# Keeping the last expert rows of the last batch on chip, in an attention and mixture-of-experts kernel

## The chip, the cores and the metric

The kernel runs on one core of a Trainium2 chip, as one launch. The core has a matrix engine (PE, with its weight loads shown as PEld), a vector engine (DVE), a scalar engine (ACT), GpSimd (POOL) and SyncE (SP), which issues DMAs. The metric is the device time of one execution in microseconds (us), as the median of several runs. Each engine takes its instructions in program order and waits on semaphores for the others.

## What is computed

A batch of four sequences of 512 tokens with 256 features passes through attention, a layernorm, a mixture-of-experts layer and a second layernorm. The layer that the change touches is this one:

```python
logits = x @ gate_w.T
topv, topi = jax.lax.top_k(logits, TOP_K)                 # 8 of 64 experts for each token
rw = softmax(topv)
W = zeros((N, E)).at[arange(N)[:, None], topi].set(rw)
gu = einsum('nh,eih->nei', x, gu_w)
gate, up = gu[..., :I], gu[..., I:]
inter_w = silu(gate) * up * W[:, :, None]
out = einsum('nei,ehi->nh', inter_w, dp_w)
out = out + sigmoid(x @ sh_gate1_w.T) * sh_out            # a shared expert
x = layernorm(x + out)
```

All of it is float32. The reference weighs every expert for every token; the kernel computes only the chosen ones.

## The kernel before

**Tiling.** A sequence is one batch b of 0 to 3; it has NT = 4 tiles of 128 tokens. The 64 experts are taken in 16 quads of four (q, 0 to 15). For one tile an expert has CELL = 32 slots, so for a batch it has SLOTS = 4 x 32 = 128 slots, and the slot is the partition of the quad's result.

**The order.** Everything is written as generators, one for each kind of work: p (project), s (scores), v (context), r (route), h (prepare), g (gather), u (up), d (down), i (fetch), c (combine) and a few small ones. The string ORDER at the top of the file has one letter for each step, and the kernel issues the steps in that order (lines 999 to 1001). The string is thus the program order on every engine; nothing else decides it. A step that stands early in the string and waits holds back what stands behind it on its engine, on that engine alone.

**Route** (line 724) makes the logits of a batch, the best eight by a max instruction, and for each chosen expert the place of the token in the expert's slots. From the place comes `code`, of which prepare and gather make one-hot matmuls that collect the tokens of 16 experts (bf16 in three parts, lines 879 to 883), and `at` (line 774), the eight row numbers of each token. The weights `w8` (lines 804 to 818) come from an exponential `rest`, picked by comparing row numbers (DVE line 808, POOL line 811, DVE line 813), with their sum `sm` for the softmax.

**Up and down.** `up` (line 893) loads the down weights of a quad (`dq`, line 897, on SP, three buffers), multiplies the collected tokens by the gate and up weights (line 907), and makes the activation on ACT and DVE (lines 914 to 916). `down` (line 920) multiplies by the down weights (line 927): the result `ys` has for each of 128 slots four experts with 256 features. ACT copies it from PSUM to `yq` (line 932), and SP stores it to `rows_out[b]` in HBM (line 934), a tensor of 8192 rows of 1 KB, where the row of a slot and an expert is `slot * 64 + expert`.

**Fetch and combine.** For every batch, tile and choice k there is one gather: 4 x 4 x 8 = 128 of them. It is an indirect DMA issued by POOL (line 945) that brings 128 rows of `rows_out[b]`, by the numbers in `at`, into one of RING = 5 buffers `got`. It has a bound check. `combine` (line 952) multiplies the rows by the weight and adds them to the tokens in place (DVE, line 956); this frees the buffer. A gather waits for all 16 stores of its batch, since the tensor is one. After every second tile, combine runs a layernorm over the pair of tiles (line 569; three rounds of Newton's method for the root) and SP stores the result (line 963).

**PSUM.** `double` takes one of three pairs of banks, `single` one of two single banks.

Of the kernel before, what the change touches and what calls it, by code (L numbers as in the profile page):

```python
# [15 lines left out]
P = 128  # L16
# [12 lines left out]
PRB = (2, 1, 1)  # L29

ORDER = (
    "pppppsppspsppppsppvvvsvsvsvvspsvvsvvsvspvsvvsvsvsvvrvvsvsrrvsvvvrhsvrrsvvsrhrsvrsprrphprppshvvvvrgpg"
    "vsvrsvhvpsrvvrrvrsvsvsvvsrsvhhvrsvvsprvsvvhrsrvrsvvgrrpprgvrpsrvgpsvrrrvrsvsvvsvvgrsrrsvvvvrrsrssrrg"
    "vhrvvvvvrgvrvtgggrruuugguugllldrruguduuggggrgdguuduggurrddguuugudgguluggduggghuhduuhdhhuhugduuggdhud"
    "gughugugdrgugdruudugguughidriiigdggcruuccgiuiicciigdggruccicuuiidiggcuuiggccrdiguucccdiugudgrgcuuiig"
    "gcdcugigghhudhuuhdughudghhuuhgduugcgduuiicggdcigcucigiudggciciccuuicggdguuiicdigchcdicuicuiguciuggdc"
    "cciuiudicccguggucicdcgugiccuiidigiuugdccciggicuiuigggcrgidghcuuhdhhuuduhicchgicucdugigiduhuugghcdugu"
    "gdgcuugdcicuuicggiccciduiuiccicidgigugcgiucgidcuicgucciidgcuiugdccgcuiiugdcccgiucgicdgicuugudcgcigcu"
    "iiggiuccciduiuiigccdicugcuccidiguiuicduudcccuciciuducuidiccuiihcidrcciicdiicizzcicicicicccccciiciicc"
    "iciicicicicicicicciiciccccicicicicicicicicicicicccccccc"  # L40
# [363 lines left out]
def kernel(  # L404
# [19 lines left out]

    nc = tc.nc
# [10 lines left out]
    ROWS = SLOTS * NE  # L436

# [16 lines left out]
    def single(name):  # L454
        return ps_s.tile([P, S], FP, tag="s", name=name)
# [41 lines left out]
    rows_out = [dram.tile([ROWS, E], FP, name=f"rows_out{i}") for i in range(B)]  # L497
# [39 lines left out]
    turn_ = const.tile([P, 1], FP, name="turn_")  # L537
    start_ = const.tile([P, 1], FP, name="start_")
    for half in range(2):
        part = slice(PART * half, PART * half + PART)  # L540
        nc.gpsimd.memset(turn_[part, :], 1.0 if half == 0 else -1.0)
        nc.gpsimd.memset(start_[part, :], 0.0 if half == 0 else float(WIDTH + 1))
    number = const.tile([P, NT, NE], FP, name="number")
    for half in range(2):
        part = slice(PART * half, PART * half + PART)
        base = NE * ((CELL - WIDTH) * half - 1) + 1
        nc.gpsimd.iota(
            number[part], pattern=[[CELL * NE, NT], [1, NE]], base=base, channel_multiplier=0,
            allow_small_or_imprecise_dtypes=True,
# [19 lines left out]
    def layernorm(r, name):  # L569

        n = r.shape[1]
        st = small.tile([P, n, 6], FP, tag=f"st{n}", name=f"st_{name}")
# [491 lines left out]
```

## Time and profile before

| what | us |
|---|---|
| median of three runs | 518.9 (517.78 to 519.8) |
| the profiled execution, own time | 567.88 |
| its span, first to last instruction | 565.9 |
| PE busy | 453.8 (80%) |
| DVE busy | 337.2 (60%) |
| ACT busy | 245.5 (43%) |
| POOL busy | 210.1 (37%) |
| start of the last down matmuls | 499.76 |
| the last gather is issued | 551.28 |
| the last store is issued | 558.75 |

The profiled execution took 49 us longer than the median of the runs; positions in the trace (in us from the span's start) belong to this execution. PE's busy time is modelled, and adds up matmuls that overlap only once. A gather's busy time is the time in which POOL writes its descriptors; the data come later. "Issue" is time for which no wait is seen. The mean clock granted to PE was 0.92 of full speed. 82.10 MB were moved by DMA.

### The profile page before, as it was taken

The numbers are of one execution on the slowest core, as the hardware profiler recorded it, in microseconds if no ns is written. First come the engines' busy times: TensorE is split into PE (matmuls) and PEld (weight loads), VectorE is DVE, ScalarE is ACT, GpSimd is POOL, SyncE is SP. The second block draws the span as 40 slices with busy tenths as digits, with TensorE's granted clock in tenths as the row PEclk, the third lists the DMA queues.
The fourth block names the chain that finished last, engine by engine and source line by source line (L and its number), as shares of the span: only waits on it lengthen the run. The fifth ranks groups of instructions, "written<-read, shape, count | busy, mean of one in ns | idle before, by whom it ended". The sixth has DMA issues, their size and how long they took to land.

```text
span 565.9 us, 12367 instructions
## 1 busy us (share of the span) xinstructions
PE 453.8 (80%) x4873; PEld 308.8 (55%) x4873; DVE 337.2 (60%) x944; ACT 245.5 (43%) x446; POOL 210.1 (37%) x233
## 2 busy tenths in 40 slices
PE   4999999999999899999879799978997876930000
PEld 2554554645555577787657586756784655720000
DVE  2233377786776884566557575665784655575543
ACT  1438666557555444565435464343553423220000
POOL 6215323433332400000563305544316354466770
PEclk9999999999999999999998899997999989885555
DMA  8700000000000085765665477673776665673331
GB/s 256 297 0 2 1 2 1 1 2 1 1 1 2 2 296 208 274 228 195 200 203 190 162 238 244 211 274 123 240 257 228 217 228 186 213 262 103 103 114 38
DMA packets 31907, 82.10 MB, mean 145 GB/s; under 512 B 4704, under 2 KB 10336, under 8 KB 30816
## 3 DMA queue, kind: packets, MB, share of 16 engines
q1 hardware_dynamic: 25696, 64.44, 32.8%
q0 software_dynamic: 6144, 16.79, 9.9%
q8 instruction: 40, 0.66, 0.5%
q14 instruction: 27, 0.22, 0.1%
HBM read 45.55 MB, written 35.65 MB: 144 GB/s over the span
## 4 chain that ended last, share of the span: by engine, by line
PE 71%; issue 7%; ACT 6%; another core or an unknown queue 5%; DVE 4%; DMA 4%; POOL 1%; POOLq 0%; SPq 0%; ACTq 0%; DVEq 0%
PE gu L907 21%; PE px L879 11%; PE y L927 10%; PE sT L653 7%; PE av L681 6%; PE pq L612 3%; PE po L715 3%; PE pk L612 3%; PE pv L626 3%; DMA got<-rows_out,at 2%; ACT pr L658 2%; PE pt_c L694 2%; ACT xt L869 2%; PE pl L736 1%
## 5 line engine op out<-in xcount | busy, mean ns | idle before, releaser
L945 POOL DMA_INDIRECT got<-rows_out,at x128 | 131.7, 1029 | 198.6 <-DVE x L956 99.7
L907 PE MATMUL gu<-xt,gu_sb 128*64 128x128 f32 x2048 | 136.2, 286 | 4.0 <-issue 3.9
L907 PEld LDWEIGHTS gu<-xt,gu_sb 128*64 128x64 f32 x2048 | 118.6, 143 | 25.5 <-issue 24.4
L658 ACT ACTIVATE pr<-sT 128x768 f32<-128x768 f32 (+1 forms) x96 | 79.3, 880 | 41.7 <-PE sT L653 41.7
L663 POOL TENSOR_SCALAR_AFFINE_SELECT pr<-pr 128x512 f32<-128x512 f32 x64 | 41.6, 661 | 109.2 <-ACT pr L658 109.2
L932 ACT COPY yq<-y 128x1024 f32<-128x1024 f32 x64 | 64.8, 1014 | 37.0 <-PE y L927 27.5
L956 DVE SCALAR_TENSOR_TENSOR x<-got,w,x 128x256 f32<-128x256 f32 x128 | 62.4, 488 | 26.3 <-DMA got<-rows_out,at 23.5
L927 PE MATMUL y<-dq,ma 64*128 64x256 f32 x512 | 72.7, 398 | 0.3 <-issue 0.2
L915 DVE SCALAR_TENSOR_TENSOR ma<-ma,gu 128x256 f32<-128x256 f32 x64 | 26.7, 418 | 73.1 <-ACT ma L914 62.5
L914 ACT ACTIVATE ma<-gu 128x256 f32<-128x256 f32 x64 | 24.6, 384 | 98.6 <-PE gu L907 42.6
L879 PE MATMUL px<-hot,xh 64*128 64x320 bf16 x256 | 40.8, 309 | 28.2 <-ACT xt L869 25.3
L869 DVE COPY xt<-px 128x512 f32<-128x512 f32 x64 | 43.8, 685 | 26.0 <-ACT xt L869 20.2
L869 ACT COPY xt<-px 128x192 f32<-128x192 f32 (+1 forms) x128 | 46.4, 375 | 26.0 <-PE px L879 17.8
L927 PEld LDWEIGHTS y<-dq,ma 64*128 64x128 f32 x512 | 48.3, 194 | 9.7 <-issue 4.5
L653 PE MATMUL sT<-qT,kT 32*128 32x128 f32 (+3 forms) x512 | 51.8, 467 | 0.5 <-ACT pr L658 0.5
L879 PE MATMUL px<-hot,xl 64*128 64x320 bf16 x256 | 41.0, 305 | 1.5 <-issue 1.5
L879 PE MATMUL px<-hot,xm 64*128 64x320 bf16 x256 | 40.5, 304 | 2.0 <-issue 2.0
L681 PE MATMUL av<-pr,va 128*32 128x128 f32 (+3 forms) x512 | 40.3, 438 | 0.3 <-POOL pr L663 0.3
L879 PEld LDWEIGHTS <-xh 64*128 64x128 bf16 x256 | 14.5, 95 | 46.1 <-issue 43.8
L653 PEld LDWEIGHTS sT<-qT,kT 32*128 32x128 f32 x512 | 24.0, 183 | 18.6 <-issue 11.7
L811 POOL TENSOR_TENSOR pick<-pick,rest 128x512 f32<-128x512 f32 x16 | 20.5, 1280 | 32.5 <-DVE pick L808 28.8
L916 DVE TENSOR_TENSOR ma<-gu,ma 128x256 f32<-128x256 f32 x64 | 27.1, 424 | 2.2
(116 smaller groups left out, 484.0 us busy)
## 6 DMA issues: line engine op xcount, KB each, us to landing
rows_out<-yq SPq DMA_DIRECT2D x64, 512.0 KB
dq<-in_dp_dram SPq DMA_DIRECT2D x64, 256.0 KB
gu_sb<-in_gu_dram SPq DMA_DIRECT2D x8, 1024.0 KB
x<-in_x_dram SPq DMA_DIRECT2D x4, 512.0 KB
got<-rows_out,at POOLq DMA_INDIRECT x128
out_dram<-x SPq DMA_DIRECT2D x8, 256.0 KB
wq_sb<-in_wq_dram SPq DMA_DIRECT2D x1, 256.0 KB
wk_sb<-in_wk_dram SPq DMA_DIRECT2D x1, 256.0 KB
```

The costliest lines, as they stand in the source:

```text
L612: nc.tensor.matmul(ps, w_sb[n][:, kc, c * P : (c + 1) * P], xT[:, kc, :], start=(kc == 0), stop=(kc == KC - 1),)
L653: nc.tensor.matmul(s_ps[r // 2][:, r % 2, lo : lo + widths[m]], kTs[b][rows, c, kb * P : (kb + 1) * P], qTs[b][rows, c, par, kb * P :], st ...
L658: nc.scalar.activation(pr[:, 2 * i : 2 * i + 2, :], s_ps[i][:, :, : sum(widths)], AF.Exp, scale=1.0 / HD**0.5)
L663: nc.gpsimd.affine_select(out=pr[:, :, lo : lo + P], in_=pr[:, :, lo : lo + P], pattern=[[0, 4], [1, P]], compare_op=ALU.is_ge, fill=0.0, ...
L681: nc.tensor.matmul(av[32 * r : 32 * r + 32, kb * P :], vas[b % 2][:, kb, 8 * c + 2 * r + par, :], pr[:, r, lo : lo + w], start=(kb == 0), ...
L869: copy(xt[:, kc, :, t * CELL + lo : t * CELL + hi], ps[:, kc, lo * GROUP : hi * GROUP].rearrange("p (s e) -> p e s", e=GROUP),)
L879: nc.tensor.matmul(ps[:, kc, first : first + WIDTH * GROUP], parts[b][i][PART * half : PART * half + PART, t, kc * P : (kc + 1) * P], o[PA ...
L907: nc.tensor.matmul(gu_ps[64 * e : 64 * e + 64, j, which, :], gu_sb[p // GUC][:, p % GUC, kc, which, 64 * e : 64 * e + 64], xt[:, kc, QUAD ...
L927: nc.tensor.matmul(ys[:, e, j, :], a[64 * e : 64 * e + 64, j, :], dq[64 * e : 64 * e + 64, j, :], start=True, stop=True,)
L932: nc.scalar.copy(yq.rearrange("s j e h -> s e j h"), ys)
L945: nc.gpsimd.indirect_dma_start(out=g, out_offset=None, in_=rows_out[b], in_offset=bass.IndirectOffsetOnAxis(ap=ats[b][:, t, k : k + 1], ax ...
L956: nc.vector.scalar_tensor_tensor(acc[:, t, :], got.pop(n), w8s[b][:, t, k : k + 1], acc[:, t, :], ALU.mult, ALU.add)
```

## The change

The last batch's last LATE = 5 quads (20 experts, q 11 to 15) are no longer stored to HBM and gathered. Their rows stay in SBUF, and a matmul adds them to the tokens. In detail:

- `rows_out` of batch 3 has only the 44 x 128 = 5632 rows of quads 0 to 10 (SOON). The row number is now `(quad * 128 + slot) * 4 + expert in the quad` in every batch, so that a quad's store is one contiguous half megabyte. Row numbers of batch 3 are clamped to SOON - 1, and the weights of the late experts are set to zero for the gathers. All 32 gathers of the batch remain.
- `route` of batch 3 makes a dense weight for all 64 experts, the total of them for the softmax (in place of `sm`), and for the late experts a pair (weight, slot number). The pair is transposed by PE, copied by ACT and written to a small HBM tensor `spread` by SP.
- `weigh` (w) reads `spread` back with four broadcasting DMAs, so that the 32 slots of each tile stand on 32 partitions with all weights and slot numbers of the tile's tokens, and DVE makes the weighted one-hot matrix `wide` in five steps.
- `down` copies a late quad into the space of the first gate and up weights, which batch 3 has used by then, and stores nothing.
- `collect` (k) multiplies `wide` by the kept rows, 80 matmuls with 32 rows, 128 columns and 256 moving columns, into two pairs of PSUM banks, and DVE adds the four results to the tokens.
- Every gather goes without a bound check.
- In batch 3 the layernorm runs over tiles 0 to 2 and then over tile 3 alone, where one operation per Newton round is merged away, and the stores of batch 3 are issued by ACT.
- ORDER is a new string throughout, 872 steps in place of 855. Ahead of the down step of batch 3's quad 10 stand 94 gathers, where it was 85; ahead of its quad 15 stand 113, where it was 94. Behind the last down step there are 15 gathers, where it was 34.

```diff
@@ ORDER: all lines replaced, the end of the string:
-    "iciicicicicicicicicciiciccccicicicicicicicicicicicccccccc"
+    "kwduuciiiciciducikddckicciwwikcizcciccckkkciiiiicciikcczccicccccikcicccc"
...
-    rows_out = [dram.tile([ROWS, E], FP, name=f"rows_out{i}") for i in range(B)]
+    rows_out = [dram.tile([ROWS if i < B - 1 else SOON, E], FP, name=f"rows_out{i}") for i in range(B)]
+    spread = dram.tile([2, NT, EL, P], FP, name="spread")
...
+        if n == 1:
+            nc.vector.tensor_scalar(ve, ve, -0.5, None, ALU.mult)
         for _ in range(3):
-            nc.vector.scalar_tensor_tensor(step, rstd, -0.5, rstd, ALU.mult, ALU.mult)
-            nc.vector.tensor_tensor(step, step, ve, ALU.mult)
+            if n == 1:
+                nc.vector.scalar_tensor_tensor(step, rstd, ve[:, 0:1], rstd, ALU.mult, ALU.mult)
+            else:
+                nc.vector.scalar_tensor_tensor(step, rstd, -0.5, rstd, ALU.mult, ALU.mult)
+                nc.vector.tensor_tensor(step, step, ve, ALU.mult)
             nc.vector.scalar_tensor_tensor(rstd, step, 1.5, rstd, ALU.add, ALU.mult)
...
-            nc.vector.scalar_tensor_tensor(row, place, float(NE), number, ALU.mult, ALU.add)
+            nc.vector.scalar_tensor_tensor(row, place, float(QUAD), number, ALU.mult, ALU.add)
...
-            nc.vector.tensor_scalar(at, near, ROWS - 1.0, None, ALU.min)
+            nc.vector.tensor_scalar(at, near, (ROWS if b < B - 1 else SOON) - 1.0, None, ALU.min)
...
+            if b == B - 1:
+                dense = lg[:, :, 0:NE]
+                nc.vector.tensor_tensor(dense, rest, chosen, ALU.mult)
+                total = small.tile([P, NT, 1], FP, tag="total", name="total", bufs=1)
+                nc.vector.tensor_reduce(total, dense, AX.X, ALU.add)
+                nc.vector.reciprocal(total, total)
+                nc.vector.memset(rest[:, :, FIRST:], 0.0)
+                yield
...
+                nc.vector.scalar_tensor_tensor(
+                    pair[:, :, 0, :], dense[:, :, FIRST:], 0.5, total.to_broadcast([P, NT, EL]), ALU.mult, ALU.mult
+                )
+                nc.vector.tensor_scalar(pair[:, :, 1, :], code[:, :, FIRST:], shift_[:, 0:1], None, ALU.add)
+                pt = single("pt_pair")
+                for t in range(NT):
+                    nc.tensor.transpose(pt[: 2 * EL, t * P : (t + 1) * P], pair[:, t].rearrange("p w e -> p (w e)"), ident)
...
+                nc.scalar.copy(flip[: 2 * EL, :], pt[: 2 * EL, :])
+                for which in range(2):
+                    nc.sync.dma_start(
+                        out=spread[which].rearrange("t e k -> e t k"),
+                        in_=flip[EL * which : EL * (which + 1), :].rearrange("e (t k) -> e t k", t=NT),
+                    )
+                yield
...
+            if b == B - 1 and q >= NQ - LATE:
+
+                n = q - (NQ - LATE)
+                yq = gu_sb[n // 2].rearrange("p g k w i -> p (g k w i)")
+                yq = yq[:, (n % 2) * QUAD * E : (n % 2 + 1) * QUAD * E]
+                nc.scalar.copy(yq.rearrange("s (j e h) -> s e j h", j=2, e=2), ys)
+                kept[n] = yq.rearrange("s (e h) -> s e h", h=E)
+                yield
+                continue
...
-            dst = rows_out[b].rearrange("(s e) h -> s e h", e=NE)
             nc.sync.dma_start(
-                out=dst[:, q * QUAD : (q + 1) * QUAD, :], in_=yq.rearrange("s j e h -> s (j e) h")
+                out=rows_out[b].rearrange("(q s e) h -> q s (e h)", s=SLOTS, e=QUAD)[q],
+                in_=yq.rearrange("s j e h -> s (j e h)"),
             )
+            yield
+
+    def weigh():
+
+        wide = hots["wide"] = late["pool"].tile([P, 2, EL, P], FP, tag="wide", name="wide")
+        for t in range(NT):
+            nc.sync.dma_start(
+                out=wide[CELL * t : CELL * (t + 1)],
+                in_=spread[:, t][None].to_broadcast([CELL, 2, EL, P]),
+            )
+        nc.vector.tensor_scalar(lane, lane, CELL - 1, None, ALU.bitwise_and)
+        nc.vector.tensor_copy(slot_, lane)
+        yield
+        for n in range(LATE):
+            part = slice(n * QUAD, (n + 1) * QUAD)
+            nc.vector.scalar_tensor_tensor(
+                wide[:, 0, part], wide[:, 1, part], slot_[:, 0:1], wide[:, 0, part], ALU.is_equal, ALU.mult
+            )
+            yield
+
+    def collect():
+
+        acc = [double(f"acc_{i}") for i in range(2)]
+        for n in range(LATE):
+            for e in range(QUAD):
+                for t in range(NT):
+                    rows = slice(CELL * t, CELL * (t + 1))
+                    nc.tensor.matmul(
+                        acc[t // 2][:, t % 2, 0:E], hots["wide"][rows, 0, n * QUAD + e, :], kept[n][rows, e, :],
+                        start=(n == 0 and e == 0), stop=(n == LATE - 1 and e == QUAD - 1), skip_group_check=True,
+                    )
+            yield
+        for t in range(NT):
+            part = xs[B - 1][:, t, :]
+            nc.vector.tensor_tensor(part, acc[t // 2][:, t % 2, 0:E], part, ALU.add)
             yield
...
-                bounds_check=ROWS - 1, oob_is_err=False,
+                bounds_check=None, oob_is_err=True,
...
-            if t % 2 and k == TOP - 1:
-                part = slice(t - 1, t + 1)
+            ends = (1, 3) if b < B - 1 else (2, 3)
+            if t in ends and k == TOP - 1:
+                part = slice(0 if t < 3 else ends[0] + 1, t + 1)
                 yield from layernorm(acc[:, part, :], f"2_{b}_{t}")
-                nc.sync.dma_start(
+                (nc.sync if b < B - 1 else nc.scalar).dma_start(
                     out=out[b].rearrange("(t p) e -> p t e", p=P)[:, part, :], in_=acc[:, part, :]
                 )
```

## The prediction

> **What bounds the kernel now.** I read the page's slices first, to see which engine is full where. The rows are PE, POOL and the clock granted to PE, each digit a tenth of a slice of 14.1 us.
>
> ```profile
> PE   4999999999999899999879799978997876930000
> POOL 6215323433332400000563305544316354466770
> PEclk9999999999999999999998899997999989885555
> ```
>
> PE is nearly full for 36 slices and empty in the last four, where POOL is at its fullest: the end is a stretch without matmuls, some 57 us long. What fills it is in the costliest groups (busy, mean ns of one, then idle before it):
>
> ```profile
> L945 POOL DMA_INDIRECT got<-rows_out,at x128 | 131.7, 1029 | 198.6 <-DVE x L956 99.7
> L932 ACT COPY yq<-y 128x1024 f32<-128x1024 f32 x64 | 64.8, 1014 | 37.0 <-PE y L927 27.5
> L956 DVE SCALAR_TENSOR_TENSOR x<-got,w,x 128x256 f32<-128x256 f32 x128 | 62.4, 488 | 26.3 <-DMA got<-rows_out,at 23.5
> ```
>
> Then the chain that ended last, around the last matmul (start, length, what):
>
> ```profile
> 499.76 1.23 PE y L927 x8
> ...
> 501.06 1.02 ACT yq L932
> ...
> 502.10 3.70 DMA rows_out<-yq
> 505.80 0.04 POOLq L945
> ```
>
> The last quad's rows are copied (1.02) and stored (3.70), and only then may batch 3's gathers start: rows_out is one tensor for a batch. The timeline dates them (start, length, idle before):
>
> ```profile
> 507.57 1.00 POOL L945 DMA_INDIRECT got<-rows_out,at  x1 [0.30 <-issue]
> ...
> 551.28 1.00 POOL L945 DMA_INDIRECT got<-rows_out,at  x1 [0.30 <-issue]
> ```
>
> These are the first and the last of its 32. They go 1.30 us apart (1.00 and 0.30 of issue), so 31 steps are 40.3 us; the other 3.4 of the 43.7 are stalls. After the last: landing and combine to 554.70, layernorm to 558.75, and the store and the end to 565.9: 14.6 us. The waits from 495 us on agree: DVE waits 22.2 us for gathers there, POOL 7.4 us for DVE. **The end is set by when batch 3's rows are complete, plus 32 gathers on POOL, plus 14.6 us.**
>
> Last, the waits between batch 2's last quad (copy at 422.92) and batch 3's quad 10 (copy at 485.72):
>
> ```profile
> POOL got L945 <- DVE x L956: 20.8, 9, 5.6
> DVE ma L915 <- ACT ma L914: 18.2, 5, 4.9
> ```
>
> POOL has room in this stretch (32.5 us busy in 62.8), and waits for ring buffers that DVE frees.
>
> **What the skill says.** Perfetto Trace Analysis, "DMA Instruction — SWDGE (GPSIMD)": the profiled window of such a DMA is the making of descriptors and not the transfer. The trace agrees: the last gather's window ends at 552.28, its combine starts at 554.22. TensorE: Matmul & The Clock Gate, "Part 1: The HAM clock gate": an idle PE falls back to half clock; the page has 0.5 in the tail. There, "Part 3: Packing small matmuls": four row tiles of 32 run at once, measured 3.07 times faster. DMA: Bandwidth & Descriptors, "Issuing engines are not separate DMA queues": another issuing engine saves only its issue time, 0.37 us for the last store here.
>
> **The change, part by part**, against the profiled execution (567.88 us, span 565.9).
>
> *Gate.* Batch 3's gathers now need quads 0 to 10 alone. Quad 10's store was issued at 486.75; with the 3.70 of the chain its rows lie at 490.45 instead of 505.80: **-15.3 us**. The five quads behind it (PE work 14.3 us of that stretch) move beside gathers. Five yq stores go; their copies, 1.01 each, stay.
>
> *Backlog.* That needs batch 2's 32 gathers out of the way. By the order string, 94 gathers stand ahead of the down step of quad 10, where before it was 85 (94 before stood ahead of quad 15). From batch 2's last rows (422.9 + 1.0 + 4.7 = 428.6) to 490.45 there are 61.9 us for 32 x 1.30 = 41.6. It fits, but nine more combines (4.4 us of DVE) and closer gathers lie among the evictions that PE waits for. I take **+2**, bounds -2 and +25 (below).
>
> *Gathers beside matmuls.* In the stretch the combines stand on DVE among ma, weighting and layernorms; a late one holds its ring buffer (five) and so POOL. Between 485.7 and 501 POOL lost 10 us this way, but then it had no haste. I take **+2.5**, bounds 0 and 8.
>
> *No bound check.* Each gather has one 29 ns register move on POOL's queue. If that alone goes, 32 x 0.03 = **-1**; if the whole 0.30 of issue goes, -9.6. No row shows a gather without it, so the lower bound is 0. I take -1.
>
> *Weights by route.* Per the nearest rows: a product and a reduction (0.43 each by L768's median), small ones at 0.18, four transposes of 0.28, one copy of 0.58, two SP stores of about 0.4 issue: some 3 us on DVE, 1 on PE, in batch 1's stretch. DVE is 60 to 66% busy there (windows 250 to 350). The two stores wait for the copy, with dq loads and row stores behind them on SP; dq has three buffers. **+0.5**, bounds 0 and 3; without that cover, about 3.
>
> *weigh.* Four broadcast loads (2.6 MB, what the five stores no longer write), then 5 x 0.7 = 3.5 us of DVE (price of L808, 128x512 with two inputs). DVE is 55% busy in the tail: 0, bounds 0 and 3.5.
>
> *collect.* 80 matmuls of 256 columns with 32 rows. L653, the same tile height, took 51.8 us for 81,920 columns, 0.63 ns each: 20,480 columns are 13 us, or 26 at half clock. Two of five groups stand ahead of the last quad. PE ends at 501 now, so at about 514 with collect, or 527 at half clock, and the end is later by 25 us or more: 0. What waits for it is four DVE additions (0.42 each). The first stand ahead of the 23rd of the 32 gathers, due at about 492.5 + 22 x 1.3 = 521; PE coming later than that would hold the combines behind them. Two of three PSUM pairs are taken meanwhile, so the last four quads alternate matmuls (0.9) with copies (1.0): hidden as well. Upper bound 6.
>
> *End.* Tile 3 is normalised alone: one statistics pass, one aggregation and one scaling fewer (0.33, 0.11, 0.33) and two small operations fewer (2 x 0.2): **-1.2**. The store is half as large, from ACT: 0, bounds -1 and +0.5.
>
> Sum: -15.3 + 2 + 2.5 - 1 + 0.5 - 1.2 = **-12.5 us**. The unprofiled runs have a median of 518.9, 49 us below the profiled execution; I can't place that difference. ACT's 3.5 us wait on an unknown queue in the moved stretch may be part of it, then the gate is worth 12. The cadence of gathers and of quads should hold, so I subtract the sum as it is: **506.4 us**.
>
> **The rivals.**
> - *Backlog rules.* Batch 2's gathers, not quad 10, set the start: the ring stalls of 20.8 us in that stretch stay, and 41.6 + 20.8 = 62.4 exceeds the 61.9 there are; in runs whose quads are quicker by a fifth, the gate comes some 12 us earlier and the backlog doesn't. Left is 2 to 8 us of gain: 511 to 516. For it: those stalls. Against: POOL was waiting for combines that stood late in the order, and the order is new.
> - *Cheap gathers.* Without the check the cadence falls by 0.2 or more, 32 times, 6 us on top: 496 to 499. For it: the 0.30 between two gathers is unexplained. Against: the one visible move is 29 ns.
> - *Slower: combines starve PE.* With gathers back to back a combine waits for its data 0.8 us, as in the tail (1.30 less 0.48); thirty of them are 25 us on DVE, ahead of the evictions of PE's PSUM. If PE loses over 1.3 us per quad in the eleven quads, 14 us, the gain is gone; at all 25, about 518.9 - 14.5 + 25 = 529. Against: up to 495 us DVE waited for gathers only 1.3 us in all.
> - *No change*: the losses just cancel the gate.
>
> **How the numbers follow.** A measurement tells 0.5% (2.6 us) from no change. The forecast (499 to 511) has 0.62; cheap gathers 0.10; backlog 0.13; no change 0.05; slower 0.10. Faster is the first three, 0.85. From 496 to 515 lies all of the forecast, nearly all of the cheap gathers and most of the backlog: 0.81. The forecast's own range is 499 to 511.
>
> **What would show it.** Right: POOL gathering batch 3 while PE still does y and gu; some 15 gathers after the last y (32 before); gathers 1.27 to 1.30 apart; batch 3's first gather soon after quad 10's store; 13 us from the last gather to the end; collect's groups done before the additions are due. Wrong: DVE waiting for gathers while PE idles before the last quad (combines starve PE); batch 3's first gather long after quad 10's rows lie there (backlog); additions waiting for PE at half clock; a cadence well under 1.2 (cheap gathers). A shift in the attention part, whose order string is new too and which I price at nothing, would also make it wrong.

## The result

| | median us | range | runs |
|---|---|---|---|
| before | 518.90 | 516.19 to 521.17 | 9 |
| changed | 515.22 | 512.76 to 516.60 | 9 |

The ratio is 0.9934, with a 95% interval of 0.9905 to 0.9963. The change makes the kernel faster by 3.7 us (0.7%), not by 12.5. The sign was right; the size was not, and 515.22 lies just above the range's upper end of 515.

One fact about the chips has to be told first. The same kernel before takes 519 us in some sets of runs and 561 to 567 us in others. The trace behind the prediction (567.88 us) is of the second sort, the times are of the first. That is the 49 us that the prediction could not place. Below, a chip is *of the first kind* where the kernel before takes 519 us and *of the second kind* where it takes 561 to 567. Whether the kind belongs to the chip for good is not known: the record gives the chips numbers, and number 2 stands for sets of both kinds (518.9 us in two, 566.1 in a later one), which may be one chip or two. Each ratio was measured on a single chip. For the first kind there is also a trace of the unchanged kernel, labelled "before, traced again", with a span of 516.1 us.

The slices of the changed kernel, first kind, one digit for 12.9 us:

```profile
PE   3999999989999989999999999999975969886700
POOL 8041412362335322000016722365633257667751
PEclk9999999999999999999999999999998899998955
```

The empty tail has shrunk to two slices, as intended. But in the 30th to 33rd slices (373 to 425 us) PE falls to 7, 5, 9 and 6. In the kernel before, traced again, it was busy 29.6 of the 30 us from 375 to 405; here 21.9. The groups (busy, mean ns of one, then idle before it):

```profile
L1033 POOL DMA_INDIRECT got<-rows_out,at x128 | 125.1, 978 | 159.9 <-DMA dq<-in_dp_dram 72.1
L1044 DVE SCALAR_TENSOR_TENSOR x<-got,w,x 128x256 f32<-128x256 f32 x128 | 62.8, 491 | 33.0 <-DMA got<-rows_out,at 31.6
L985 ACT COPY yq<-y 128x1024 f32<-128x1024 f32 x59 | 59.7, 1013 | 48.0 <-PE y L971 35.6
```

A gather is 49 ns shorter (1027 ns in the trace of before on the first kind). Next, the first and the last of batch 3's 32 gathers on the timeline. The kernel before, traced again:

```profile
459.49 1.00 POOL L945 DMA_INDIRECT got<-rows_out,at  x1 [0.76 <-DVE x L956]
...
501.80 0.99 POOL L945 DMA_INDIRECT got<-rows_out,at  x1 [0.30 <-issue]
```

The changed kernel:

```profile
460.11 0.94 POOL L1033 DMA_INDIRECT got<-rows_out,at  x1 [2.42 <-DMA dq<-in_dp_dram]
...
503.84 0.95 POOL L1033 DMA_INDIRECT got<-rows_out,at  x1 [0.30 <-issue]
```

**Batch 3's first gather starts no earlier than before**, although it now needs quad 10 alone. Quad 10 itself has moved. The copy of its rows in the kernel before, traced again, and in the changed kernel:

```profile
434.69 1.01 ACT L932 COPY yq<-y 128x1024 f32<-128x1024 f32 x1 [0.73 <-PE y L927]
```

```profile
454.57 1.01 ACT L985 COPY yq<-y 128x1024 f32<-128x1024 f32 x1 [0.72 <-PE y L971]
```

Times in us from the span's start; "small loads" is an experiment below:

| | before, again | changed | small loads |
|---|---|---|---|
| batch 2's quad 5 copied | 353.56 | 356.18 | 356.21 |
| batch 2's quad 10 copied | 374.05 | 373.57 | 374.53 |
| batch 3's quad 10 copied | 434.69 | 454.57 | 446.41 |
| batch 3's quad 15 copied | 453.73 | 481.51 | 474.71 |
| first gather of batch 3 | 459.49 | 460.11 | 452.05 |
| last gather | 501.80 | 503.84 | 495.15 |
| span | 516.06 | 514.76 | 505.81 |

In the kernel before, 19.0 us lay between quad 10 and quad 15. In the changed kernel quad 10 comes 19.9 us later, so the whole gate is used up. What is left is the end: from the last gather to the span's end it was 14.3 us and is 10.9.

The chain of the changed kernel shows where part of it went (start, length, what):

```profile
383.55 1.01 ACT yq L985
...
384.59 13.34 DMA rows_out<-yq
...
398.03 1.02 ACT yq L985
...
399.10 2.08 PE y L971 x8
```

A row store takes 13.34 us to land; in the prediction's chain it took 3.70. Meanwhile ACT can't copy the next quad, since both yq buffers are taken, and PE waits for PSUM. Ahead of this store, at 375.5 to 377.4, stand the four loads of `weigh`:

```profile
wide<-spread SPq DMA_DIRECT2D x4, 640.0 KB, 11.2
```

That is 2.62 MB, and the prediction had priced it at nothing.

### The profile page after: what moved, and what is told of

It reads as the page before. It is cut to its first block, busy times and chain, and to the rows that moved or that the text cites. A ratio compares the mean times of both kernels' runs of the same rounds, so it can differ in the third digit from the quotient of the medians.

```text
span 514.8 us, 12588 instructions
## 1 busy us (share of the span) xinstructions
PE 446.6 (87%) x5037; PEld 306.5 (60%) x5037; DVE 343.7 (67%) x957; ACT 246.4 (48%) x447; POOL 204.3 (40%) x236
## 2 busy tenths in 40 slices
DMA packets 31688, 82.20 MB, mean 160 GB/s; under 512 B 4708, under 2 KB 10500, under 8 KB 30340
## 4 chain that ended last, share of the span: by engine, by line
PE 59%; DMA 19%; DVE 10%; ACT 6%; issue 4%; POOL 1%; SPq 0%; POOLq 0%; DVEq 0%; ACTq 0%
DMA got<-rows_out,at 15%; PE gu L951 14%; PE sT L669 7%; PE y L971 7%; PE av L697 7%; PE px L923 7%; PE pv L642 3%; PE po L731 3%; PE pq L628 3%; ACT pr L674 3%; DMA rows_out<-yq 3%; PE pk L628 2%; DVE x L1044 2%; PE pt_c L710 2%; POOL got L1033 1%
## 5 line engine op out<-in xcount | busy, mean ns | idle before, releaser
L1033 POOL DMA_INDIRECT got<-rows_out,at x128 | 125.1, 978 | 159.9 <-DMA dq<-in_dp_dram 72.1
L951 PE MATMUL gu<-xt,gu_sb 128*64 128x128 f32 x2048 | 126.5, 277 | 1.5 <-DVE xt L913 1.0
L951 PEld LDWEIGHTS gu<-xt,gu_sb 128*64 128x64 f32 x2048 | 111.1, 137 | 20.6 <-issue 16.1
L985 ACT COPY yq<-y 128x1024 f32<-128x1024 f32 x59 | 59.7, 1013 | 48.0 <-PE y L971 35.6
L971 PE MATMUL y<-dq,ma 64*128 64x256 f32 x512 | 71.4, 398 | 12.5 <-ACT yq L985 4.1
L971 PEld LDWEIGHTS y<-dq,ma 64*128 64x128 f32 x512 | 46.8, 192 | 23.6 <-issue 6.1
L913 DVE COPY xt<-px 128x512 f32<-128x512 f32 x64 | 43.7, 684 | 17.9 <-ACT xt L913 17.8
L923 PE MATMUL px<-hot,xh 64*128 64x320 bf16 x256 | 39.4, 302 | 11.5 <-ACT xt L913 5.7
L923 PE MATMUL px<-hot,xl 64*128 64x320 bf16 x256 | 39.0, 298 | 0.0
L923 PE MATMUL px<-hot,xm 64*128 64x320 bf16 x256 | 38.9, 297 | 0.0
L697 PEld LDWEIGHTS av<-pr,va 128*32 128x32 f32 x512 | 13.9, 109 | 26.5 <-issue 18.4
```

The lines of the kernel that those rows point to most:

```text
L697: nc.tensor.matmul(av[32 * r : 32 * r + 32, kb * P :], vas[b % 2][:, kb, 8 * c + 2 * r + par, :], pr[:, r, lo : lo + w], start=(kb == 0), ...
L913: copy(xt[:, kc, :, t * CELL + lo : t * CELL + hi], ps[:, kc, lo * GROUP : hi * GROUP].rearrange("p (s e) -> p e s", e=GROUP),)
L923: nc.tensor.matmul(ps[:, kc, first : first + WIDTH * GROUP], parts[b][i][PART * half : PART * half + PART, t, kc * P : (kc + 1) * P], o[PA ...
L951: nc.tensor.matmul(gu_ps[64 * e : 64 * e + 64, j, which, :], gu_sb[p // GUC][:, p % GUC, kc, which, 64 * e : 64 * e + 64], xt[:, kc, QUAD ...
L971: nc.tensor.matmul(ys[:, e, j, :], a[64 * e : 64 * e + 64, j, :], dq[64 * e : 64 * e + 64, j, :], start=True, stop=True,)
L985: nc.scalar.copy(yq.rearrange("s j e h -> s e j h"), ys)
```

## The experiments

The theory after the result (**bytes**): the loads stand among transfers that the quads need, and delay the gate. The rival (**order**): the new string puts combines and other DVE work among the evictions, and PE waits for those. Before this was clear there were other suspects: the burst, the pace of POOL, and the bound check.

**First runs, chips of the second kind.** The kernel before, unchanged, for its trace:

> The kernel before once more, unchanged, to have a trace of it beside the changed kernel's. Theory: the 49 us by which its profiled execution exceeded its runs were waits of ACT on an unknown queue (37 us in the first trace) between 250 and 500 us; without them the last down matmuls end near 455 us, the tail of 65 us stays as it was (gathers 1.30 us apart), and the span is about 517 us. Rival: the tail itself is shorter in an ordinary run, below 55 us, and PE ends later than 462.

It took 565.43 us. The changed kernel with hardly any load (the string has one letter w more, for the memset, ahead of the first down step):

```diff
         wide = hots["wide"] = ...
+        nc.gpsimd.memset(wide, 0.0)
+        yield
         for t in range(NT):
-            nc.sync.dma_start(out=wide[CELL * t : CELL * (t + 1)], in_=spread[:, t][None].to_broadcast([CELL, 2, EL, P]))
+            nc.sync.dma_start(out=wide[CELL * t : CELL * (t + 1), :, 0:1],
+                              in_=spread[:, t, 0:1][None].to_broadcast([CELL, 2, 1, P]))
```

> The changed kernel with 0.13 MB in place of the 2.6 MB that weigh loads: only one of 20 experts is read back, the rest of the weights is filled with zeros by POOL while it idles, so the late experts' part is left out of the output. Theory (the burst): the four loads hold up the row stores behind them, which stopped PE for about 8 us and slowed batch 3's first quads; without them 502 to 507 us. Rival (the backlog of gathers): the end is set by 64 gathers of batches 2 and 3 on POOL and in the ring, and the burst is absorbed; 513 to 515.

The loads apart (a `yield` behind each load, and the letters w behind the down steps 31, 35, 39 and 43):

> The changed kernel with its four weigh loads (0.66 MB each) issued one at a time, behind the down steps 31, 35, 39 and 43, in place of all four at once behind step 43. Same bytes. Theory (the burst): what hurts is that a store waits behind four loads; apart, each delays a store by under 3 us, which two buffers cover: 504 to 509 us. Rival (the bytes): DMA is so full in this stretch that 2.6 MB more cost 8 to 10 us wherever they stand: 513 to 517. Rival (the backlog): 513 to 515 as well, together with the small load.

The bound check put back:

```diff
-                bounds_check=None, oob_is_err=True,
+                bounds_check=(ROWS if b < B - 1 else SOON) - 1, oob_is_err=False,
```

> The changed kernel with the bound check of the gathers put back. In the traces a gather took 0.998 us with it and 0.95 without (medians), both with 0.30 between. Theory: 0.05 us on each of the 32 gathers at the end, so 1.6 us longer, 516 to 518. Rival: off the path, since gathers in the ring wait for their data anyway: within 0.5 us of 515.2.

The changed kernel itself, and the loads apart once more:

> The changed kernel itself. The first four runs fell on a chip on which the kernel before takes 565 us, not 518.9, and in whose trace PE's semaphore increments arrive 3 to 15 us late while POOL issues gathers one after another. If this call falls on such a chip, theory: the changed kernel is slower than before by about 1%, 569 to 573, since it puts more back to back gathers beside matmuls; rival: it gains its 4 us there too, 560 to 562. On a chip like the one of the result: 513 to 517 against 519.

> The four loads of weigh one at a time (behind the down steps 31, 35, 39 and 43), once more, beside the unchanged changed kernel. On a chip like the one of the result: theory (the burst), 504 to 509; rivals (the bytes, or the backlog), 513 to 517. On the other kind of chip the order of the two should be the same, with less between them, since late increments hide part of it.

| kernel | us | ratio to before (95%) |
|---|---|---|
| small loads | 570.14 | 1.0072 (1.0048 to 1.0097) |
| loads apart | 569.89 | 1.0085 (1.004 to 1.0131) |
| bound check back | 571.95 | 1.0109 (1.0037 to 1.018) |
| changed kernel, second chip | 566.94 | 1.0094 (1.0056 to 1.0132) |
| loads apart, second chip | 567.58 | 1.0107 (1.0039 to 1.0176) |

All five are alike within their intervals, and slower than before. The changed kernel, faster by 0.7% on the first kind, is slower by 0.9% here. Its trace on such a chip shows a wait that the first kind doesn't have. One of ACT's waits over the span, then PE, POOL and ACT on the timeline:

```profile
ACT ma L958 <- remote: 34.4, 5, 14.0
```

```profile
500.18 3.94 PE L951 MATMUL gu<-xt,gu_sb 128*64 128x128 f32 x64
```

```profile
503.13 0.94 POOL L1033 DMA_INDIRECT got<-rows_out,at  x1 [0.30 <-DVE st L586]
...
514.50 0.94 POOL L1033 DMA_INDIRECT got<-rows_out,at  x1 [0.30 <-issue]
```

```profile
517.35 0.38 ACT L958 ACTIVATE ma<-gu 128x256 f32<-128x256 f32 x1 [13.97 <-remote]
```

The trace has the end of PE's gate and up product at 504.12. ACT, which waits for it, starts at 517.35. In the 13.2 us between, POOL issues gathers back to back, and PE's semaphore increment for this product is on record only at 517.33, behind the last of them. PE itself is slow there: collect's next 32 matmul records run from 504.05 to 518.54, 14.5 us, and the same group takes 2.01 on the first kind. So it isn't told whether the increment alone is late or PE as a whole is held up, and that the gathers are the cause is not shown. "Remote" is the trace's word for a releaser that it does not find. The kernel before has the same on the second kind (ACT ma waits 37.1 us for "remote" in the prediction's trace, 30.9 in the one taken here). On the first kind neither trace has one such wait. That five kernels which differ in loads and check come out alike here may be because this waiting covers what they differ in; no run separates the two. What was asked had to be asked on the first kind.

**POOL's pace, and the loads apart, first kind.** One small memset behind each gather, meant to slow POOL down; then the loads apart; and the kernel before for its trace:

```diff
                 bounds_check=None, oob_is_err=True,
             )
+            nc.gpsimd.memset(idle, 0.0)
             yield
```

> The changed kernel with one more POOL instruction, a memset of 128x1, behind each of its 128 gathers. On a chip like the one of the result: POOL takes 0.1 to 0.3 us more for each gather; if the cadence of gathers sets the end (theory of the backlog), the last 32 to 64 of them make it 4 to 12 us longer; if the ring, DVE or PE do (rival), it stays within 2 us. On a chip like the two of the first runs: theory, PE's increments pass in the pauses, and the kernel comes down from 567 towards 530; rival, they wait for something else than POOL's series, and it stays at 567 to 575.

> The four loads of weigh one at a time, for the third time; wanted on a chip like the one of the result. There: theory (the burst), 504 to 509; rivals (the bytes, or the backlog), 513 to 517. On the other kind of chip as before: the same as the changed kernel.

> The kernel before, unchanged, for its trace on this chip. If before is at 519 here, theory: its last down matmuls end near 455 us and its tail is about 60 us; the last gather is issued some 45 us behind the last down step. Rival: PE ends later than 462, and the tail is shorter than 55 us.

The memset: 514.6, ratio 0.993 (0.9907 to 0.9954), as without it. But it slowed nothing: its 0.12 us fell into the 0.30 between two gathers, and their starts still lie 1.25 apart in its trace, so the run doesn't tell whether POOL's pace sets the end. Whether a longer pause lets PE's increments pass on the second kind was not tried there. The loads apart: 517.22, ratio 0.9969 (0.995 to 0.9989), no better than in one burst (0.9934, and the intervals overlap). Quad 10 is copied at 454.00, where in one burst it was 454.57. Row stores took 5.35 us on average to land from 330 to 374 (4.09 in the changed kernel), dq loads 6.90 (4.73): the harm is spread, not gone. So it is not the burst as such that costs. The kernel before took 517.96.

**The loads, taken out, moved, and put alone into the kernel before; first kind, on one chip.**

> The changed kernel with 0.13 MB read back in place of the 2.6 MB (one late expert of twenty has its weights, the others are multiplied by zeros, so that the late experts' part is left out); the order string, the gathers and the matmuls are the same. Where the kernel before takes 519 us: if the bytes of the four loads hold back the transfers that the matmuls wait for (theory: bytes), quad 10 of batch 3 is copied some 9 us earlier than in the changed kernel, at about 445, and the time is 505 to 509 (ratio to before 0.973 to 0.981). If the new order with its earlier combines is what delays the matmuls (rival: order), nothing moves: 513 to 516, ratio 0.99 to 0.996. Where before takes 561 to 565, the late semaphore increments of PE cover both: 1.005 to 1.01.

For the second, only the string differs: the load's w stands behind the down step 59 (batch 3's quad 10), the five DVE steps and collect behind it; the two letters w that stood ahead of that step are gone from there.

```diff
@@ ORDER, from the d of quad 10 on
-diiigggucidcicicicccciciuuciciccwiuuccikwduuciiiciciducikddckicciwwikcizcciccckkkciiiiicciikcczccicccccikcicccc
+dwiiigggucidcicicicccciciuucicicciuucciduuciiiciciduciwdwdkwckicciwkiwckizcciccckkkciiiiicciikcczccicccccikcicccc
```

> The changed kernel with the four loads moved behind the down step of quad 10, and the five steps of DVE and the groups of collect moved behind them; nothing is left out. Theory (bytes): the loads no longer stand among the transfers that the quads need before the gate, so quad 10 is copied at about 445 as without the loads, batch 3's first gather starts at 449 to 452, and the time is 505 to 510, unless the additions of collect come later than the combines that stand behind them, which would cost up to 5. Rival (order): quad 10 stays at 452 to 455 and the time at 513 to 517. Where before takes 561 to 565: a ratio of 1.0 to 1.01.

The third adds four such loads to the kernel before, from a stretch of x, ahead of the down step 44:

```diff
+    def load():
+        wide = late["pool"].tile([P, 20, E], FP, tag="wide", name="wide")
+        for t in range(NT):
+            nc.sync.dma_start(out=wide[CELL * t : CELL * (t + 1)],
+                              in_=x[0, 20 * t : 20 * t + 20, :][None].to_broadcast([CELL, 20, E]))
+        yield
```

> The kernel before with four broadcasting loads of 640 KB each added ahead of the down step of batch 2's quad 11, where the changed kernel has them; what they bring is not used. Theory (bytes): 2.6 MB at the 270 to 280 GB/s that move in this stretch are 9.4 us; the transfers take 85% of the DMA engines there, so the quads up to quad 15 of batch 2 come 6 to 10 us later and the time is 525 to 529 (ratio 1.012 to 1.02). Rival (order): the buffers hide the loads, and the time is 518 to 520.5 (ratio 0.998 to 1.003). Where before takes 561 to 565: a ratio of 1.0 to 1.015 by the theory.

| kernel | us | ratio to before (95%) |
|---|---|---|
| small loads | 507.07 | 0.9774 (0.9735 to 0.9813) |
| loads behind quad 10 | 517.71 | 0.9985 (0.9959 to 1.001) |
| before, with the loads added | 535.00 | 1.0295 (1.0259 to 1.033) |

Without the loads the changed kernel takes 507.07, 0.7 us from the forecast. The loads are worth 1.6% (0.9934 less 0.9774), 8.3 us, or 5.8 to 10.8 with both intervals; in the traces quad 10 moves by 8.2. The wait behind the store is gone. ACT's copies, first in the changed kernel, then with small loads:

```profile
386.76 1.00 ACT L985 COPY yq<-y 128x1024 f32<-128x1024 f32 x1
398.03 1.01 ACT L985 COPY yq<-y 128x1024 f32<-128x1024 f32 x1 [7.87 <-DMA rows_out<-yq]
```

```profile
387.74 1.00 ACT L985 COPY yq<-y 128x1024 f32<-128x1024 f32 x1
391.23 1.01 ACT L985 COPY yq<-y 128x1024 f32<-128x1024 f32 x1
```

Put alone into the kernel before, the loads cost 16.5 us, more than the 6 to 10 expected. PE stood still for one dq load that stood behind them. Its waits from 375 to 412:

```profile
ACT yq L932 <- PE y L927: 19.1, 5, 16.7
...
PE y L927 <- DMA dq<-in_dp_dram: 14.9, 1, 14.9
```

The bytes alone, 2.62 MB at 270 to 280 GB/s, would be 9.4 us by the estimate made ahead of the run. That the rest comes from the order in the queue is argued, not shown. The Trainium skill, DMA: Bandwidth & Descriptors, "Queues, rings and completion order", says that SP's transfers stand in one ring per DMA engine and are taken from it in order, and that an engine serves the rings of different issuers in turn. The trace fits the first: dq loads issued at 374 to 404 took 17.97 us on average to land, 4.51 without the added loads. But POOL's gathers, in another ring, slowed nearly as much, from 4.25 to 14.56, so the trace doesn't tell the order in a ring from a plain lack of room on the DMA engines. A load from another ring was not tried.

Behind quad 10 the loads hurt as much, in another place. The gate did move (quad 10 copied at 445.42, first gather at 451.12), but the next eight gathers took 18.5 us where with small loads they took 10.2. The waits from 450 to 472:

```profile
PE y L971 <- DMA dq<-in_dp_dram: 16.1, 1, 16.1
DVE x L1044 <- DMA got<-rows_out,at: 12.5, 5, 7.1
```

My expectation of 505 to 510 was wrong there: I had taken the stretch behind the gate for an idle one, and it holds the gathers that set the end.

**Half the bytes, and the matmul steps' order; first kind, on one chip.** Slot and weight become one number, slot plus weight, and a weight is below one:

```diff
-                nc.vector.tensor_scalar(pair[:, :, 1, :], code[:, :, FIRST:], shift_[:, 0:1], None, ALU.add)
+                nc.vector.scalar_tensor_tensor(pair, code[:, :, FIRST:], shift_[:, 0:1], pair, ALU.add, ALU.add)
...
-                in_=spread[:, t][None].to_broadcast([CELL, 2, EL, P]),
+                in_=spread[t][None].to_broadcast([CELL, EL, P]),
...
+        nc.vector.tensor_scalar(slot_, slot_, -1.0, None, ALU.mult)
...
-                wide[:, 0, part], wide[:, 1, part], slot_[:, 0:1], wide[:, 0, part], ALU.is_equal, ALU.mult
+            nc.scalar.activation(wide[:, part], wide[:, part], AF.Relu, bias=slot_[:, 0:1], scale=1.0)
+            nc.vector.scalar_tensor_tensor(wide[:, part], wide[:, part], 1.0, wide[:, part], ALU.is_lt, ALU.mult)
```

> The changed kernel with slot number and weight added up to one number (slot plus weight), so that the four loads bring 1.31 MB in place of 2.62; ACT takes the own slot off with a Relu and DVE keeps what is below one. Nothing is left out and the order string is the changed kernel's. Theory (bytes): the loss scales with the bytes, so half of the 8 us between the changed kernel and the one with small loads comes back: 510 to 512 where before takes 519 (ratio 0.983 to 0.988); quad 10 of batch 3 copied at about 450. Rival: what costs is the first burst or the count of loads, and the time stays at 514 to 516 (ratio 0.991 to 0.995). Where before takes 561 to 565: 1.0 to 1.01 by either.

The second kernel mixes the strings: the start up to the first down steps and h, g and u from the string of before (but for one h, ten down steps earlier), fetch, combine, weigh, collect and the last steps of route from that of the changed kernel.

> As the kernel with half the bytes, with the order string mixed: prepare, gather-matmul, up and down steps (h, g, u) stand between the down steps as in the kernel before; fetch, combine, weigh, collect and the last steps of route stand between them as in the changed kernel. It tells where the other 11 to 12 us before quad 10 come from (quad 10 at 446 without the loads, 435 in the kernel before). If they come from the arrangement of the matmul steps, quad 10 comes at 438 to 441 and the time is 500 to 505 where before takes 519 (ratio 0.964 to 0.973). If they come from the earlier gathers and combines beside matmuls, quad 10 stays near 450 and the time is within 2 us of the half-bytes kernel (510 to 513), or above where the mixed string fits its buffers worse. Where before takes 561 to 565: 0.99 to 1.01.

**Half the bytes take 509.17 us, ratio 0.9807 (0.9768 to 0.9846): faster than both kernels, and nothing is left out.** Half the bytes cost only 0.33% (0.9807 less 0.9774), 1.7 us, where in proportion to the bytes it would be 4. With both intervals the cost may be anything up to 4.6, so that the loss grows faster than the bytes is suggested and not shown. The traces point the same way: quad 10 is copied at 446.41 with small loads, 448.93 with half the bytes and 454.57 with all. That buffers hide the loads up to some amount would fit; no run shows it. The kernel with half the bytes also has one store less, and ACT has five steps more. Its four loads of 320 KB landed in 7.1 to 8.6 us, the four of 640 KB in the changed kernel in 9.3 to 17.2.

The mixed order took 528.15, ratio 1.0212 (1.0165 to 1.0259), beyond the numbers of both expectations; the second had left room for a string that fits its buffers worse. ACT waits 13.8 us for DVE's `left` of prepare between batch 2's quad 5 and 15, where the kernel with half the bytes waits 4.4. The mixture made a delay of its own, so it settles nothing on the order.

**The picks early, all of it early.** In the half-bytes kernel the last steps of batch 3's route (r 58 to 62) are moved behind the down steps 25 to 33. In the second kernel, r 54 to 57 also go behind the steps 8 to 12, r 58 to 62 behind 18 to 28, and the loads behind step 15.

> The half-bytes kernel with one thing moved in the order string: the last five steps of route for batch 3 (four picks with their sums, 1.4 us of DVE each, and the scaling) stand behind the down steps 25, 27, 29, 31 and 33, at 300 to 335 us, where they stood behind 37, 43, 48, 50 and 57. In the trace of the kernel with small loads PE idles 10.8 us between batch 2's quad 5 and batch 3's quad 10, where before it idled 2.4, and DVE does 72.3 us of work there where before it did 61.3. If this DVE work ahead of the gate is what PE waits for (theory), the 5.6 us moved out bring 3 to 5 us: 504 to 506.5 where before takes 519 (ratio 0.971 to 0.977). If the waits come from where the combines stand (rival), or from the DMA queues, nothing comes of it: 508 to 510 (0.979 to 0.984). Where before takes 561 to 565: 0.99 to 1.01 by either.

> As the kernel with the picks early, and more: batch 3's weights and pair (route steps 54 to 57) stand behind the down steps 8 to 12, the picks behind 18 to 28, and the four half-size loads behind step 15, at 260 to 270 us, where the DMA engines are busy 70% and no gather runs yet. Theory (bytes and cover): the loads then hold back nothing that the end waits for; beside the gain of the picks another 1.5 to 2.5 us: 502 to 505 (ratio 0.968 to 0.974), with a bend of up to 2 us at batch 0's quad 15. Rival: the loads cost the same there, since PE is full and waits for the same stores and weights: as the kernel with the picks early, within 1 us. Where before takes 561 to 565: 0.99 to 1.01.

> The half-bytes kernel with the four picks and the scaling of batch 3's weights moved to 300 to 335 us, once more, for a chip where the kernel before takes 519. Theory (the DVE work ahead of the gate is what PE waits for): 504 to 506.5, ratio 0.971 to 0.977. Rival (place of the combines, or the queues): 508 to 510, ratio 0.979 to 0.984. Where before takes 561 to 567 the first try gave 1.017, and another such result tells nothing on this question.

> The kernel with the picks, the pair and the half-size loads early (260 to 270 us), once more, for a chip where the kernel before takes 519. Theory: 502 to 505, ratio 0.968 to 0.974. Rival: within 1 us of the kernel with the picks early alone. Where before takes 561 to 567 the first try gave 1.027.

Both tries fell on chips of the second kind: 1.0171 (1.0121 to 1.0221) and 1.0196 (1.0164 to 1.0228) for the picks, 1.0267 (1.0221 to 1.0312) and 1.0287 (1.0248 to 1.0326) for all early. On such a chip they come out worse than the changed kernel (1.0094, 1.0056 to 1.0132), the first of them only at the edge of the intervals. In the second trace with the picks early one of PE's increments again comes 13.6 us late beside gathers issued back to back. On the question that they were made for they say nothing.

## Why the prediction was wrong, point by point

**The failed step: weigh's loads at 0.** The prediction put it as "2.6 MB, what the five stores no longer write". The total is indeed the same (82.10 and 82.20 MB). But the stores left the stretch from quad 11 on, and the loads came into batch 2's quads 10 to 15, ahead of the gate, where the DMA engines were busy 80% and row stores and dq loads stand behind them that PE needs. Cost: 8.3 us, shown by the small loads. The prediction named a bound for weigh (0 to 3.5) and put only DVE's work into it. For the loads it gave neither a place nor cover, although the string says that they stand between batch 2's quad 10 and 11. Added up from the two traces of the first kind, the gate is worth -19.0 us (quad 10 to quad 15 in the kernel before); the loads cost 8.2 and the rest of what delays quad 10 costs 11.7; from quad 10's copy to the first gather it is 0.2 less, the 31 steps of the gathers are 1.4 longer and the end is 3.3 shorter. That makes -1.3, the difference of the two spans; the medians differ by 3.7.

**Backlog, +2.** This was too small by far, and that the kernel without loads comes out at the forecast is luck: the terms cancel. The gate with the backlog should bring the first gather 13.3 us forward. With small loads it comes 7.4 earlier (459.49 to 452.05), although the gate is worth 19.0 on the first kind in place of 15.3. So 11.7 us are eaten before quad 10 (446.41 less 434.69). They are lost behind batch 2's quad 10, which is copied at 374.53 with small loads and at 374.05 before. The next quad's copy comes 10.0 us later with small loads, and 2.9 before: 7 of the 11.7 us arise there, in a stretch where PE is busy 6.8 us of the 10. The rival "Slower: combines starve PE" had the right place, PE's waits in that stretch, and by the rows below the wrong cause. The windows from batch 2's quad 5 to batch 3's quad 10 (stretch, length; busy PE, PEld, DVE, ACT, POOL; clock, DMA share, GB/s), for before traced again, small loads and the changed kernel:

```profile
353.56:434.69 81.13, 78.72 (x1089) 61.95 (x1084) 61.26 (x154) 45.17 (x92) 45.42 (x45) 1.00 0.84 280
```

```profile
356.21:446.41 90.20, 79.44 (x1070) 62.34 (x1068) 72.33 (x187) 44.04 (x88) 49.39 (x51) 1.00 0.77 257
```

```profile
356.18:454.57 98.39, 81.27 (x1070) 63.38 (x1068) 72.73 (x187) 43.89 (x88) 50.91 (x51) 0.97 0.83 261
```

PE does nearly the same work. It idles 2.4, 10.8 and 17.1 us. Without the loads it still idles 8.4 us more than before, and DVE does 11.1 us more there: three more picks of batch 3 with their sums (4.1), one more pair of layernorm, the shared expert's additions (1.7), two more combines. All of it stands before batch 3's combines, so it comes ahead of the earlier gate. PE's waits in the kernel with small loads, same stretch:

```profile
PE px L923 <- ACT xt L913: 4.0, 8, 1.0
PE y L971 <- DVE ma L960: 2.2, 1, 2.2
PE px L923 <- DVE xt L913: 1.7, 1, 1.7
```

These waits are for evictions of PSUM and for activations, not for gathers. DVE waited for gathers 6.4 us, less than the 11.6 before. That the moved DVE work is the cause of PE's waits is argued from these rows and not shown: on the second kind the runs made for it could not tell. What stays open is how the 11.7 us divide between DVE's added work and the place of the steps.

**Attention and weights by route, 0 and +0.5.** The prediction named a shift in the attention part as a sign of being wrong. There is none: batch 0's first quad is copied at 206.86 us before and at 206.09 in the changed kernel. And since batch 2's quad 10 is not late either (374.05 and 373.57), no cost of the route's new steps is to be seen up to there.

**Gate, -15.3.** The mechanism was right: the first gather starts 5.8 us behind quad 15's copy in the kernel before, and 5.5, 5.6 and 5.7 behind quad 10's in the changed kernel, with small loads and with the loads behind quad 10. Its premise failed: the step counted from quad 10's place in the old trace, as if nothing ahead of it moved. With the loads and the order, it comes 19.9 us later.

**Gathers beside matmuls, +2.5.** 31 steps took 43.7 us on the first kind (42.3 before), with 1.25 us between the starts in place of 1.30. Without stalls that is 38.8, and 5.0 are stalls (2.0 before): 3 us more, close to the +2.5.

**No bound check, -1.** The window of a gather is 1027 ns with it and 978 without: 32 x 0.049 = 1.6 us. The 0.30 of issue stays, so "cheap gathers" is refuted. What is saved lies in the window in which POOL writes descriptors, not in the register move. In the time it could not be seen (1.0109 with it and 1.0094 without, on different chips).

**weigh's DVE steps and collect, hidden.** The DVE steps were 0.745 us each, five are 3.7 (3.5 predicted). Collect's matmuls took 9.8 us of PE, 0.48 ns for a column (13 us and 0.63 ns predicted). The packing that the prediction names shows in the trace: four matmuls of 32 rows start within 20 ns of each other, and the next four 216 ns later. PE ends at 487.17, 16.7 before the last gather: no addition waits for PE. Right.

**The end, -1.2.** It was -3.3. From the last combine's start to the store's issue, with the single tile's layernorm, it is 0.9 shorter (4.53 to 3.62), nearly as predicted. The rest, 2.4, lies between the store's issue and the end of the span (6.85 to 4.45), where the bound was -1. How much of it is the smaller store and how much the other engine was not tried.

**The rivals.** "Backlog rules" gave 511 to 516 and by its number came nearest, but not by its mechanism: batch 2's last gather starts at 456.75, 3.4 us ahead of batch 3's first, much as before (1.8). Quad 10 and the backlog came late together. The 49 us that could not be placed should have widened the range: they were the sign that trace and times were of two kinds.

## What to carry to other kernels

A transfer is priced by what stands behind it. The same bytes, moved from the stretch behind quad 10 (DMA engines 78% busy in the kernel before) into one ahead of it (80% busy), cost 8 us here, so the busy share does not give the price. Moving them behind the gate only moved the wait. Halving the bytes by packing two numbers into one won back 6 us for a few instructions. Where a gate is moved forward, all work that the order puts before it comes along, and its room on each engine and queue has to be counted ahead of the gate. And where a trace's own time is far from the measured ones, each step should be asked whether it rests on waits of that one execution.

## What was not expected of the hardware

- The same kernel has two levels of time, 519 and 561 to 567 us, and the change is a gain of 0.7% at the first and a loss of 0.9% at the second. In the changed kernel's trace at the second, one increment of PE's semaphore is on record 13.2 us behind the matmul's end while POOL issues gathers back to back, and PE needs 14.5 us there for matmuls that take 2.0 at the first. At the first, no increment in the traces of the kernel before and the changed one was over 1 us late. What makes the difference is not known.
- Four loads of 640 KB, each spreading one 20 KB block over 32 partitions, landed in 9.3 to 17.2 us in the changed kernel. Two row stores of 512 KB issued behind them took 13.3 and 12.5 us, where they take 3.7 on average in the kernel before.
- With half of these bytes quad 10 came 2.5 us later than with almost none, with all of them 8.2 us later.
